# A two-layer mixture-of-experts kernel: where the shared experts of the last two token segments stand, and how the last result is stored

## The chip, the cores and the metric

The kernel runs on one core of one Trainium2 chip, in one launch. The metric is the device time of that launch in microseconds; smaller is better. The kernel before takes 1428.38 us (median of 3 runs, 1427.42 to 1430.12).

A core has TensorE (PE, matmuls and transposes; PEld is its weight load), VectorE (DVE), ScalarE (ACT), GpSimd (POOL) and SyncE (SP), each with a queue of instructions of its own that it works off in order, and 16 DMA engines. Here SP issues the loads and the output stores, ACT the writes of finished pages, and POOL the indirect transfers.

## The reference, cut to what matters

The input is x of 4 x 1024 x 256 (4096 tokens, D = 256), all in float32. Four blocks follow one another, each on a layer norm of x and added to x: an RWKV mixer, a mixture of experts, a retention mixer, and the same mixture of experts again with the same weights. The change lies in the last block:

```python
logits = flat @ router_w
scores = jax.nn.softmax(logits, axis=-1)
_, topk_idx = jax.lax.top_k(logits + router_bias, K)             # K = 4 of E = 64
...
g = silu(einsum('nd,edf->nef', flat, wg));  u = einsum('nd,edf->nef', flat, wu)
routed = einsum('ne,nef,efd->nd', comb, g * u, wd)               # F = 64 per expert
sg = silu(einsum('nd,sdh->nsh', flat, swg)); su = einsum('nd,sdh->nsh', flat, swu)
shared = einsum('nsh,shd->nd', sg * su, swd)                     # 2 x 256 hidden, every token
return (routed + shared)
```

So each token passes four of 64 small routed experts and, besides, two shared experts that see every token.

## The kernel before, in words

**Tiling.** The 4096 tokens are 8 segments (`NSEG`) of 512, each 4 tiles of 128 (`TT`). x stays in SBUF for the whole kernel as eight tiles `xs[i]` of 128 x 4 x 256. The routed experts work on pages: 128 rows that belong to one expert. Tokens are sent to rows of a buffer `sent` in HBM by indirect DMAs; a pair of pages at a time is loaded, worked on and written to a buffer `made`; then each tile of tokens gathers its four rows from `made` and adds them to x with their weights. In the usual case, which this input takes, there are 83 pairs, numbered 0 to 82.

**The routed steps** (`routed`). Step p issues `load(p)` (on SP: 256 KB of rows `rx_f` and two times 192 KB of weights `rw_f`), `up` of pair p-2 (four transposes `rt_f`, L542, copied by VectorE, L546), `mid` of pair p-3 (eight matmul records `rg_f`, L554; silu on ScalarE, L559; product on VectorE, L562) and `down` of pair p-4 (`rp_f`, L574; copied out on ScalarE, L581, and written to `made` by a DMA on ACT's queue, L582). Rows and weights have 6 buffers, finished pages 4.

**The shared experts** (`shared(i)`). Six steps per segment: four `up` (each 4 matmul records `g_f` and 4 `u_f`, L457, silu on ScalarE, L462, product on VectorE, L463) and two `down` (each 16 records `o_f`, L470, and an add to two tiles of x on VectorE, L475). The hidden activations `sh_f` have one buffer, the result of a `down` has one PSUM buffer, and `g_f`, `u_f` and `rg_f` share four.

**The gathers** (`gather`, `gathers`). For each tile four indirect DMAs on POOL (`gy_f`, L606), and `LAG` = 7 positions later four adds on VectorE (L617). A gather waits for the latest "beat", one of the products or copies L463, L546 and L562 that was emitted before it (`on_beat`), and for the pages it may read. Segment i may read the pages up to `until(i)`: 33, 38, 43, 51, 59, 67, 75 and 83 pairs.

**The order.** `track(steps, lo, hi)` spreads a list of steps evenly over positions from `lo` to `hi`, where a position is a step of the routed loop, and `merge` sorts all steps by position and emits them. The builder then orders the instructions of each engine within what the dependencies allow; the adds of a gather and the gathers keep the order in which they were emitted. In `second_layer` the shared experts of segments 0 to 2 are already done (`BESIDE` + `FILL` = 3). Those of segments 3 to 6 are spread over positions 0.5 to n - 4 with n = 83, those of segment 7 over n - 3 to n + 11. A store of a segment (L1253) stands behind the adds of its last tile. The gathers of segment 7 stand at 86.5 to 94.5, its adds at 93.5 to 101.5.

Of the kernel before, what the change touches and what calls it, by code (L numbers as in the profile page):

```python
# [25 lines left out]
TT = SEG // P  # L26
# [22 lines left out]
def track(steps, lo, hi):  # L49

    return [(lo + (hi - lo) * n / len(steps), step) for n, step in enumerate(steps)]


def merge(*tracks):

    for _, step in sorted((s for t in tracks for s in t), key=lambda s: s[0]):
        step()
# [3 lines left out]
def hybrid_kernel(ctx: ExitStack, tc: tile.TileContext, a: dict, out: bass.AP):  # L61
    nc = tc.nc
    B, T, _ = a["x"].shape
    N = B * T
    NSEG = N // SEG
# [27 lines left out]
    def seg_dram(t, i):  # L93
        b, s = divmod(i, SPB)
        return t[b, s * SEG : (s + 1) * SEG, :].rearrange("(t p) d -> p t d", p=P)
# [5 lines left out]
    def bank(tag, name, shape=None):  # L101
# [9 lines left out]
    xs = [const.tile([P, TT, D], F32, name=f"x{i}") for i in range(NSEG)]  # L111
# [7 lines left out]
        out=upper, in_=ones, compare_op=ALU.is_ge, fill=0.0, base=-1,  # L119
# [41 lines left out]
    PACE, LAG = 2, 7.0  # L161
# [1007 lines left out]
    BESIDE, FILL = 0, 3  # L1169
# [14 lines left out]
    def first_layer(until):  # L1184
# [16 lines left out]
        with right("turned") as pt:  # L1201
# [38 lines left out]
            with tc.tile_pool(name="pr2", bufs=2, reuse_waits="tile") as pr:  # L1240
                f2.in_order(
                    lambda u: second_layer(f2, pr, u), pairs_until if until is pairs_until else None
                )
        arm.close()

    def second_layer(f2, pr, until):

        side, stores = [], []
        for i in range(BESIDE + FILL, NSEG - 1):
            side += f2.shared(i)  # L1250
        gathers = f2.gathers(pr, until)
        for i in range(NSEG):
            store = lambda i=i: nc.sync.dma_start(out=seg_dram(out, i), in_=xs[i])  # L1253
            stores.append((gathers[2 * i + 1][-1][0] + 0.1, store))

        n = until(NSEG - 1)
        merge(
            f2.routed(pr, until), *gathers, stores, track(side, 0.5, n - 4),
            track(f2.shared(NSEG - 1), n - 3, n + 4 + LAG),
        )  # L1260

    f1.in_order(first_layer)
# [63 lines left out]
```

## Time and profile before

| what | value |
|---|---|
| median of 3 runs | 1428.38 us (1427.42 to 1430.12) |
| profiled execution, its time | 1426.64 us |
| its span from first to last instruction | 1424.7 us |
| mean granted TensorE clock | 0.954 |
| TensorE busy | 1260.2 us, 88% of the span |
| VectorE, ScalarE, GpSimd busy | 994.2, 738.6, 529.9 us |
| first matmul of the second layer's routed pairs | 1107.43 us |
| last matmul record | 1398.13 us, 3.72 us long |
| last gather issued, last add | 1415.38 us, 1418.22 us |

Times inside an execution count from the start of its span. "Busy" is the time in which an engine works on an instruction; a wait counts as idle and is put down to what ended it. Names such as `rg_f<-rxT_f,rw_f` read "output <- inputs" with the buffer numbers left out, and L554 is line 554 of the kernel before. In tables by stretches of time each engine has its busy time and, in brackets, its number of instructions; behind them stand the granted clock as a share of full speed, the mean busy share of the 16 DMA engines (slightly over 1 where packets overlap) and the bytes moved.

### The profile page before, as it was taken

The page shows a single profiled execution, that of the slowest core. Times are in us where ns is not written, and L with a number is a line of the kernel's source. Part 1 is how long each engine was busy: PE and PEld are TensorE (multiplying, and loading weights), DVE is VectorE, ACT ScalarE, POOL GpSimd, SP SyncE. Part 2 cuts the span into 40 slices and gives each one's busy share as a digit, 9 for nine tenths or more (in the row PEclk, how much of TensorE's full clock was granted, in tenths as well). Part 3 has the DMA queues.
Part 4 walks back from the last instruction along what each step waited for, and adds up shares of the span by engine and source line. Part 5 has one row for each costly group of instructions (what it writes and reads, how often), then busy time and mean ns, then how long its engine had stood idle before and what let it go on. Part 6 is the DMA issues. An engine that isn't in the chain of part 4 may idle for free. (4 is left out here: it accounts for less than half of the span.)

```text
span 1424.7 us, 23821 instructions
## 1 busy us (share of the span) xinstructions
PE 1260.2 (88%) x7872; PEld 891.4 (63%) x7872; DVE 994.2 (70%) x2510; ACT 738.6 (52%) x1422; POOL 529.9 (37%) x536
## 2 busy tenths in 40 slices
PE   6789999999389979998998999799997899999993
PEld 2455555556277767776776666566464687777772
DVE  6999989998355547775777788866673355486664
ACT  7989888973134455555654463433331234454440
POOL 0043255536400155432334105536717000376565
PEclk9999999999789999998999999799999899999997
DMA  9985931112399996765552101212202898999984
GB/s 350 403 254 74 297 115 60 60 37 82 123 310 349 336 331 211 235 206 195 164 187 91 36 31 68 74 38 79 100 16 103 260 318 278 324 384 378 363 310 128
DMA packets 192297, 276.26 MB, mean 194 GB/s; under 512 B 53795, under 2 KB 119718, under 8 KB 192166
## 3 DMA queue, kind: packets, MB, share of 16 engines
q1 hardware_dynamic: 143686, 163.98, 36.1%
q0 software_dynamic: 24576, 67.14, 14.2%
q10 hardware_dynamic: 23904, 43.53, 8.1%
q8 instruction: 65, 1.06, 0.3%
q14 instruction: 66, 0.54, 0.1%
HBM read 166.05 MB, written 121.11 MB: 202 GB/s over the span
## 5 line engine op out<-in xcount | busy, mean ns | idle before, releaser
L429 POOL DMA_INDIRECT sent<-xn_f,to_f x256 | 278.2, 1087 | 415.3 <-issue 192.9
L606 POOL DMA_INDIRECT gy_f<-made,to_f x256 | 248.6, 971 | 468.9 <-DVE rh_f L562 143.3
L554 PE MATMUL rg_f<-rxT_f,rw_f 128*128 128x128 f32 x1328 | 186.6, 283 | 8.4 <-DVE rxT_f L546 2.9
L554 PEld LDWEIGHTS rg_f<-rxT_f,rw_f 128*128 128x128 f32 x1328 | 165.9, 194 | 19.7 <-DVE rxT_f L546 11.6
L559 ACT ACTIVATE rs_f<-rg_f 64x256 f32<-64x256 f32 x166 | 62.4, 376 | 218.9 <-PE rg_f L554 187.4
L542 PE MATMUL rt_f<-ident,rx_f 128*128 128x128 f32 x664 | 107.2, 285 | 45.3 <-DMA rx_f<-sent 41.5
L574 PE MATMUL rp_f<-rw_f,rh_f 64*128 64x128 f32 x1328 | 137.9, 300 | 6.9 <-DVE rh_f L562 3.6
L546 DVE COPY rxT_f<-rt_f 128x512 f32<-128x512 f32 x166 | 114.2, 688 | 39.5 <-PE rt_f L542 37.9
L581 ACT COPY ry_f<-rp_f 128x256 f32<-128x256 f32 x266 | 92.8, 374 | 90.8 <-DMA made<-ry_f 40.3
L617 DVE SCALAR_TENSOR_TENSOR x<-gy_f,w_f,x 128x256 f32<-128x256 f32 x256 | 122.1, 480 | 14.6 <-DMA gy_f<-made,to_f 10.8
L457 PE MATMUL g_f<-xnT_f,f_swg 128*128 128x512 f32 x256 | 130.7, 627 | 0.6 <-ACT sh_f L462 0.6
L470 PE MATMUL o_f<-f_swd,sh_f 128*128 128x256 f32 x512 | 121.5, 385 | 8.2 <-DVE sh_f L463 4.2
L574 PEld LDWEIGHTS rp_f<-rw_f,rh_f 64*128 64x128 f32 x1328 | 102.1, 186 | 34.9 <-ACT ry_f L581 8.7
L457 PE MATMUL u_f<-xnT_f,f_swu 128*128 128x512 f32 x256 | 122.2, 595 | 0.7 <-DVE sh_f L463 0.7
L542 PEld LDWEIGHTS rt_f<-ident,rx_f 128*128 128x128 f32 x664 | 76.2, 144 | 69.4 <-issue 34.1
L562 DVE TENSOR_TENSOR rh_f<-rg_f,rs_f 64x256 f32<-64x256 f32 x166 | 70.6, 426 | 64.9 <-ACT rs_f L559 61.8
L470 PEld LDWEIGHTS o_f<-f_swd,sh_f 128*128 128x128 f32 x512 | 94.9, 190 | 30.0 <-DVE sh_f L463 6.7
L683 PE MATMUL rvk<-xnT_a,rvk 128*128 128x512 f32 x192 | 91.5, 623 | 7.9 <-DVE xnT_a L240 7.4
L1060 DVE TENSOR_TENSOR pm<-sc,decay 128x512 f32<-128x512 f32 x128 | 83.8, 681 | 8.3 <-PE sc L1039 7.1
L463 DVE TENSOR_TENSOR sh_f<-u_f,sh_f 128x512 f32<-128x512 f32 x64 | 43.7, 685 | 62.5 <-PE u_f L457 56.3
L462 ACT ACTIVATE sh_f<-g_f 128x512 f32<-128x512 f32 x64 | 38.0, 596 | 90.7 <-PE g_f L457 50.9
L457 PEld LDWEIGHTS u_f<-xnT_f,f_swu 128*128 128x128 f32 x256 | 48.1, 191 | 57.1 <-issue 52.6
(238 smaller groups left out, 2178.0 us busy)
## 6 DMA issues: line engine op xcount, KB each, us to landing
rw_f<-wx SPq DMA_DIRECT2D x332, 192.0 KB
rx_f<-sent SPq DMA_DIRECT2D x166, 256.0 KB
made<-ry_f ACTq DMA_DIRECT2D x166, 256.0 KB
sent<-zeros SPq DMA_DIRECT2D x7, 2048.0 KB
sent<-zeros SPq DMA_DIRECT2D x1, 10240.0 KB
x<-in_x_dram SPq DMA_DIRECT2D x8, 512.0 KB
wx<-in_wg_dram SPq DMA_DIRECT2D x2, 2048.0 KB
sent<-xn_f,to_f POOLq DMA_INDIRECT x256
```

The costliest lines, as they stand in the source:

```text
L429: ins = nc.gpsimd.indirect_dma_start(out=rows_sent[: pairs_until(i) * 2 * P, :], out_offset=bass.IndirectOffsetOnAxis(ap=st["to"][:, c : c ...
L457: nc.tensor.matmul(ps, lhsT=w[:, k, s], rhs=self.xnT[i][:, k, :], start=(k == 0), stop=(k == KC - 1),)
L470: nc.tensor.matmul(o[:, t, :], lhsT=st["h"][:, c, s], rhs=self.weights[2][:, c, :], start=(c == 0), stop=(c == NS - 1),)
L542: nc.tensor.transpose(tp[:, k, j, :], s["x"][:, j, k * P : (k + 1) * P], ident)
L546: beat(nc.vector.tensor_copy(out=xT, in_=tp))
L554: nc.tensor.matmul(gu[:, j, :], lhsT=s["w"][:, j, k * 2 * F : (k + 1) * 2 * F], rhs=s["xT"][:, k, j, :], start=(k == 0), stop=(k == KC - 1),)
L574: nc.tensor.matmul(yp[:, j, :], lhsT=s["h"][r, j, :], rhs=s["w"][r, j, WD:], start=True, stop=True,)
L581: copy(out=y[:, :, c * P : (c + 1) * P], in_=yp)
L606: ins = nc.gpsimd.indirect_dma_start(out=got[t][:, k, :], out_offset=None, in_=rows_made[: ready[t] * 2 * P, :], in_offset=bass.IndirectOf ...
L617: tc.keep_in_program_order(nc.vector.scalar_tensor_tensor(out=xs[i][:, t, :], in0=got[t][:, k, :], scalar=s["w"][:, c : c + 1], in1=xs[i][ ...
L683: nc.tensor.matmul(ps, lhsT=rvk[:, k, lo : lo + P], rhs=st["xnT"][:, k, :], start=(k == 0), stop=(k == KC - 1),)
L1060: ins = nc.vector.tensor_mul(out=pm, in0=ch[j]["sc"][g], in1=decay.rearrange("p (k g b) n -> p g k b n", k=KC, b=2)[:, g],)
```

## The change

In the second layer only. The shared experts of segment 6 leave the spread-out list (which then holds segments 3 to 5, 18 steps instead of 24, over the same positions) and get positions n + 2 to n + 6, 85 to 89, around and behind the last steps of the routed loop. Those of segment 7 move from n - 3 ... n + 11 to n + 6 ... n + 10, 89 to 93. The store of the last segment becomes four stores of one tile (128 KB) each, every one behind the adds of its tile; the other segments are still stored whole.

```diff
         side, stores = [], []
-        for i in range(BESIDE + FILL, NSEG - 1):
+        for i in range(BESIDE + FILL, NSEG - 2):
             side += f2.shared(i)
         gathers = f2.gathers(pr, until)
         for i in range(NSEG):
-            store = lambda i=i: nc.sync.dma_start(out=seg_dram(out, i), in_=xs[i])
-            stores.append((gathers[2 * i + 1][-1][0] + 0.1, store))
+
+            each = [slice(t, t + 1) for t in range(TT)] if i + 1 == NSEG else [slice(0, TT)]
+            for t in each:
+                store = lambda i=i, t=t: nc.sync.dma_start(
+                    out=seg_dram(out, i)[:, t, :], in_=xs[i][:, t, :]
+                )
+                stores.append((gathers[2 * i + 1][t.stop - 1][0] + 0.1, store))
+
 
         n = until(NSEG - 1)
         merge(
             f2.routed(pr, until), *gathers, stores, track(side, 0.5, n - 4),
-            track(f2.shared(NSEG - 1), n - 3, n + 4 + LAG),
+            track(f2.shared(NSEG - 2), n + 2, n + 6), track(f2.shared(NSEG - 1), n + 6, n + 10),
         )
```

In the list of changes the work is the same: the same matmuls, adds and bytes, three more output transfers.

## The prediction

> **What bounds the kernel now.** I read four views. First the page, for which part of the span the change touches: the last nine slices (from about 1104 us) are the second layer.
>
> ```profile
> PE 1260.2 (88%) x7872; PEld 891.4 (63%) x7872; DVE 994.2 (70%) x2510; ACT 738.6 (52%) x1422; POOL 529.9 (37%) x536
> ...
> PE   6789999999389979998998999799997899999993
> ...
> DMA  9985931112399996765552101212202898999984
> GB/s 350 403 254 74 297 115 60 60 37 82 123 310 349 336 331 211 235 206 195 164 187 91 36 31 68 74 38 79 100 16 103 260 318 278 324 384 378 363 310 128
> ```
>
> TensorE and the DMA engines are both full there, and both go idle together in the last slice. Which of the two would give way is the question. Second, the table of busy time in stretches of 10 us (PE, PEld, DVE, ACT, POOL, then clock, DMA share, GB/s):
>
> ```profile
> 1160.00:1170.00 10.00, 10.00 (x83) 8.07 (x82) 6.34 (x13) 4.61 (x12) 0.00 (x0) 1.00 0.92 293
> ...
> 1260.00:1270.00 10.00, 10.00 (x72) 7.31 (x71) 9.37 (x20) 5.23 (x14) 7.85 (x8) 1.00 1.05 392
> ...
> 1290.00:1300.00 10.00, 7.58 (x44) 5.40 (x44) 4.31 (x9) 4.10 (x11) 7.56 (x9) 0.83 1.03 368
> ...
> 1340.00:1350.00 10.00, 8.57 (x60) 7.33 (x59) 6.12 (x13) 4.48 (x12) 5.58 (x7) 1.00 1.00 337
> ...
> 1400.00:1410.00 10.00, 1.85 (x9) 1.29 (x7) 6.76 (x15) 0.00 (x0) 7.87 (x8) 0.80 0.54 158
> ```
>
> Three regimes. Until about 1220 TensorE is full and the DMA moves 260 to 330 GB/s. From there (gathers have begun) to 1370 TensorE is still full and the DMA moves 355 to 392, with two dips; the thirteen rows from 1240 to 1370 have a mean of 375.5 GB/s and a share between 1.00 and 1.06. From 1392 TensorE runs dry. Third, the chain of waits at the end:
>
> ```profile
> 1387.88 0.89 PE rg_f L554 x8
> ...
> 1393.89 3.47 PE o_f L470 x16
> ...
> 1398.50 0.95 POOL gy_f L606
> ...
> 1415.38 2.75 DMA gy_f<-made,to_f
> ...
> 1418.22 0.48 DVE x L617
> ```
>
> After the last pair's pages are made, sixteen gathers of the last segment go out, one every 1.25 us, then an add and a store: the end is POOL's, and TensorE idles in it. Fourth, TensorE's own timeline there, with the work that the change moves:
>
> ```profile
> 1386.00 1.88 PE L457 MATMUL u_f<-xnT_f,f_swu 128*128 128x512 f32 x4
> 1387.72 1.05 PE L554 MATMUL rg_f<-rxT_f,rw_f 128*128 128x128 f32 x8
> 1388.70 0.72 PE L574 MATMUL rp_f<-rw_f,rh_f 64*128 64x128 f32 x8
> 1389.35 1.13 PE L457 MATMUL g_f<-xnT_f,f_swg 128*128 128x512 f32 x2
> ...
> 1398.13 3.72 PE L470 MATMUL o_f<-f_swd,sh_f 128*128 128x256 f32 x16 [0.78 <-DVE x L475]
> ```
>
> The row at 1387.72 is `rg_f` of the last pair (82). From its start to the end of the span is 37.0 us. I use it as the mark: the change makes the way to it shorter and the way from it longer.
>
> **The way to the mark, if TensorE sets it.** One `up` of a shared expert costs 2 x 1.72 us (the spacing of its groups), one `down` 3.45 (16 matmuls in 3.47), a segment 20.7. In the order in which TensorE gets its instructions, seven `up` and two `down` that now stand ahead of the mark stand behind it afterwards: 7 x 3.44 + 2 x 3.45 = 31.0 us. Of these 10.3 (one `up`, two `down`) are already gone at pair 40, whose `rg_f` starts at 1239.64, because 18 shared steps instead of 24 are spread over the same pairs. TensorE alone would reach the mark at 1356.7.
>
> **If the DMA sets it.** The trace's DMA packets have the weights of pair 40 landed at 1233.2 and those of pair 82 at 1375.5, with 53.0 MB moved between (48.8 in the thirteen rows, 4.2 at the edges). The weights lie 6.4 us ahead of `rg_f` at pair 40 and 12.2 at pair 82. Afterwards pair 40 is there at 1222.9 if the first regime gives its 10.3: there the DMA has room: a pair takes 3.19 us now (`rp_f` of pair 10 at 1151.1, of pair 33 at 1224.4), a shared step every 4.36 instead of 3.27 positions takes 0.26 off, and 293 x 3.19/2.93 = 319 GB/s is less than the 355 and more seen later. In the second regime TensorE wants 148.1 - 20.7 = 127.4 us for these 42 pairs; 53.0 MB in that is over 410 GB/s, more than any row. So TensorE catches up with the loads, and the pages and gathers of the three pairs by which it now trails move in that stretch too: 3 x 576 KB (256 written, 256 gathered, 64 stored) = 1.7 MB. 54.7 MB at the mean of 375.5 take 145.7: mark at 1368.6, 19.1 earlier instead of 31.0. Bounds: at 372.4, this stretch's own 53.0 MB in 142.3 us, 1369.8; at 392, the best row, 1362.4; at TensorE's own pace 1356.7. I take the mean and not the best row because what makes the dips (a page write that waits for an output store, a store that holds SP's queue) stays in the program.
>
> **The way from the mark.** By the new order: `rg_f` 0.98, `rp_f` 0.65, two `up` 6.88, the last `rp_f` 0.65, two `up` 6.88, two `down` with the 0.78 wait for their one PSUM buffer 7.68, four `up` 13.76 less one matmul of 0.43 that fits in that wait, two `down` 7.68; 0.32 until VectorE starts: 45.1. VectorE's queue has all sixteen adds of the last segment behind the second `down`'s add: 0.61 + 16 x 0.50 = 8.6. Then the store: 6.0 from the last add to the end now (1418.70 to 1424.70), with 512 KB in packets from 1419.64 to 1421.32; a quarter of them takes 0.42, so 4.7. The bounds for that store are 4.3 (no packets) and 6.0 (nothing saved). Sum 58.4, which is 21.4 more than now.
>
> What hides what: the last pair's page lands some 3.6 us after its `rp_f` (1391.05 to 1394.6), so sixteen gathers at 1.25 plus 2.75 would be over about 27 us behind it; TensorE and its adds take 36 and more, so the gathers no longer end anything. POOL's last six gathers now wait for the last `up` (a gather waits for the latest beat), and still land 6 us before their adds are due. The adds of segment 6 stand between the multiplies of the shared `up` in VectorE's queue; their gathers go out pair by pair some 10 us ahead, as now. SP is moved past nothing: the stores of segments 5 to 7 stand behind the last load in both programs, four issues of 0.4 us instead of one, three of them during the adds. ACT's `silu` of the moved `up` (0.60) lies beside matmuls of 3.44.
>
> **Sum.** +21.4 - 19.1 = +2.3. To this comes the clock: after the 2.33 us wait before 1295.94 the row's clock is 0.83, and eight `rp_f` took 1.60 instead of 0.72 and four `g_f` 3.27 instead of 1.98, 2.2 us in all. A TensorE that waits for loads will meet this about once more (bounds: none, and three times): +4.5. The profiled execution took 1426.64 for a span of 1424.7, the median of the runs is 1.74 above that; on the median 1428.38 this gives 1432.9.
>
> Two rules set beside these rows. The Trainium skill, "DMA: Bandwidth & Descriptors", section "Where 436 GB/s comes from", puts the ceiling at 435 GB/s by the ports and at about 358 where HBM binds: by 358 the mark would be at 1375.7 and the sum +9.4, by 435 TensorE would set the pace and the sum be -9.6. The rows of 375 to 392 already exceed the lower figure, so the measurement decides. "TensorE: Matmul & The Clock Gate", section "What's actually happening", lets the clock fall only after an idle window of about 3.4 us; by that the short waits for loads would cost no clock and the sum would be +2.3, but the row shows a fall after a wait of 2.33.
>
> **The rivals.** (A) The DMA engines carry more than they are asked for now, and it gets faster. For: rows of 392 stand next to each other, and the loads land 6 to 12 us before use. Against: the share does not rise above 1.06. It decides at 54.7 MB / (1366.3 - 1222.9) = 381 GB/s; at 392 the end is 3.9 earlier (1424.5), at TensorE's pace 9.6 earlier (1418.8). (B) The first regime gives nothing, because a DMA share of 0.9 is already its limit at 293 GB/s. Against: the row of 1150 to 1160 moves 373. It would cost up to 10.3 more: 1443. (C) VectorE stalls in the tail: an add of segment 6 whose gather is late stands before a multiply that frees TensorE's PSUM banks. Each microsecond late is one more; with four gathers late (5 us) 1438. For it speaks that POOL runs without a break from 1372 on now.
>
> **Chances.** My case 0.50 (1427 to 1437; slower 0.41, within 0.09), A 0.32 (faster 0.28, within 0.04), B 0.11 and C 0.07 (slower). Within means 0.2%, 2.9 us, about what a measurement of this kernel can tell from no change. So faster 0.28, same 0.13, slower 0.59. The range leaves out TensorE's full pace at one end and the whole of B at the other: 1420 to 1441.
>
> **What would show it.** Right: the last `rg_f` near 1368, 54 to 60 us before the end; GB/s between 1230 and 1360 like today's mean; gaps on TensorE before `rg_f` that loads end; all sixteen `x` adds of the last segment without gaps behind the last L475; a last chain through `o_f` and `u_f` in place of POOL. Wrong: rows above 385 throughout and the mark before 1364 (A), pair 40 not earlier than 1236 (B), L463 waits in the tail ended by a gather (C).

## The result and the profile after

| | kernel before | changed kernel |
|---|---|---|
| median of 16 runs each | 1431.18 us (1419.49 to 1441.13) | 1435.76 us (1431.78 to 1440.81) |
| profiled execution, its time and span | 1426.64 us, 1424.7 us | 1434.38 us, 1432.6 us |
| `rg_f` of pair 40, of pair 82 (the mark) | 1239.64, 1387.72 us | 1229.9, 1371.37 us |
| from the mark to the end of the span | 37.0 us | 61.3 us |
| last `x` add ends, from there to the end | 1418.70 us, 6.0 us | 1425.47 us, 7.2 us |

The ratio is 1.0044, 95% interval 1.0025 to 1.0064: the changed kernel is slower by 6.3 us (3.6 to 9.2) by the ratio and by 4.6 us between the medians, where 4.5 were forecast. A ratio, here and below, leaves out the executions in a slower state and so is not quite that of the two medians (1.0032 here). The two profiled executions lie 7.7 us apart; that of the kernel before is 4.5 us under its median here, that of the changed kernel 1.4 under its own. The sums below are made between the profiles.

First the page of the changed kernel, its 40 slices.

```profile
PE   6789999999298879998998999789996999988895
...
DMA  9986931112599986766453011112203899999952
GB/s 349 403 252 79 295 108 59 59 41 78 169 314 335 318 305 211 234 209 214 145 188 90 25 46 67 59 49 86 81 33 112 298 315 342 369 386 360 368 192 69
```

In the kernel before, TensorE and the DMA engines went idle together in the last slice. Now the DMA engines go quiet in the last two slices (192 and 69 GB/s) while TensorE works on there (its digits are 9 and 5, where the last one was 3): the shared experts stand behind the last loads. The table in stretches of 10 us (PE, PEld, DVE, ACT, POOL, then clock, DMA share, GB/s) shows the same and one thing more.

```profile
1160.00:1170.00 10.00, 9.70 (x88) 8.38 (x85) 6.25 (x13) 5.04 (x14) 0.00 (x0) 1.00 0.99 340
...
1260.00:1270.00 10.00, 9.82 (x65) 7.06 (x64) 6.82 (x14) 5.20 (x14) 7.56 (x9) 1.00 1.06 396
...
1300.00:1310.00 10.00, 8.40 (x48) 7.18 (x48) 4.25 (x9) 3.23 (x10) 4.21 (x5) 0.67 1.01 349
...
1350.00:1360.00 10.00, 6.65 (x62) 5.69 (x60) 5.34 (x11) 4.03 (x12) 6.32 (x7) 1.00 1.05 384
...
1400.00:1410.00 10.00, 10.00 (x27) 4.88 (x26) 3.66 (x7) 1.79 (x3) 3.50 (x4) 1.00 0.19 51
```

The first regime has become faster (340 GB/s in this row where it had 293; the seven rows from 1150 to 1220 have a mean of 325 after 303). The second moves about what it moved before, but TensorE is no longer full in it: it waits, and the row from 1300 has a mean granted clock of 0.67. In the trace's record of the clock this mean is half the clock from 1299.91 to 1303.32 and again from 1306.74, and the full clock between. The last row is the new tail, TensorE alone. TensorE's own timeline shows the mark and the end of the tail:

```profile
1371.37 1.16 PE L554 MATMUL rg_f<-rxT_f,rw_f 128*128 128x128 f32 x8
1372.46 0.89 PE L574 MATMUL rp_f<-rw_f,rh_f 64*128 64x128 f32 x8
...
1413.19 3.72 PE L470 MATMUL o_f<-f_swd,sh_f 128*128 128x256 f32 x16 [0.78 <-DVE x L475]
```

VectorE's timeline from there has the second `down`'s add and then all sixteen adds of the last segment in one block:

```profile
1416.94 0.69 DVE L475 TENSOR_TENSOR x<-o_f,x 128x512 f32<-128x512 f32 x1 [3.81 <-PE o_f L470]
1417.55 7.91 DVE L617 SCALAR_TENSOR_TENSOR x<-gy_f,w_f,x 128x256 f32<-128x256 f32 x16
```

No gather is waited for. POOL's chain at the end of the kernel before is gone, and its place is taken by the matmuls.

Where TensorE waits in the middle, the chain of waits (start, length, what was waited for) runs through transfers:

```profile
1288.10 8.35 DMA rx_f<-sent
1296.47 7.22 DMA rw_f<-wx
1303.77 5.07 DMA made<-ry_f
1308.91 4.15 DMA made<-ry_f
```

I had expected TensorE to wait for its weights. It does not: by the packets, the weights of pair 60 have landed at 1292.7 and its `rg_f` starts at 1299.3, those of pair 82 at 1366.0 and 1371.4. Nor is a transfer named in the list of its waits from pair 40 to the mark (what waited, for what; us in total, times, longest), of which these are the first three lines:

```profile
PE rp_f L574 <- DVE rh_f L562: 6.2, 4, 3.4
PE rt_f L542 <- DVE rxT_f L546: 4.9, 6, 1.9
PE rt_f L542 <- ACT ry_f L581: 0.9, 1, 0.9
```

What waits for transfers is ScalarE, in order, as its timeline around two of the stalls shows (ACTq is the issue of a page write):

```profile
1303.77 0.33 ACTq L582 DMA_DIRECT2D made<-ry_f  x1
1304.14 0.38 ACT L559 ACTIVATE rs_f<-rg_f 64x256 f32<-64x256 f32 x1 [4.11 <-PE rg_f L554]
...
1358.25 0.33 ACTq L582 DMA_DIRECT2D made<-ry_f  x1
1358.63 0.38 ACT L559 ACTIVATE rs_f<-rg_f 64x256 f32<-64x256 f32 x1 [4.78 <-DMA out_dram<-x]
```

The page write at 1303.77 goes out when the weight load issued at 1296.47 has landed (7.22 us, the second line of the chain), the one at 1358.25 when an output store has. The trace shows why: the transfers of SyncE and ScalarE take eight completion semaphores in turn, in the order of the program, and a transfer waits for the one eight before it, whatever that is. (The page write at 1303.77 has the semaphore of that weight load, whose last update came at 1303.69.) The `silu` of the next pair (`rs_f`) stands behind the page write on ScalarE, `rh_f` on VectorE and `rp_f` on TensorE behind that. The first of the two stalls is put down to `rg_f`, which had ended at 1300.6: a label names what came last by the profile, and is not always what was waited for.

There is a second path, by the copies `rxT_f`, which stand on VectorE behind adds that wait for their gathers. One of TensorE's waits for them is this (1.30 us):

```profile
1270.80 0.88 DVE L617 SCALAR_TENSOR_TENSOR x<-gy_f,w_f,x 128x256 f32<-128x256 f32 x2 [1.06 <-DMA gy_f<-made,to_f]
1271.71 0.69 DVE L546 COPY rxT_f<-rt_f 128x512 f32<-128x512 f32 x1
1272.46 0.66 PE L542 MATMUL rt_f<-ident,rx_f 128*128 128x128 f32 x4 [1.30 <-DVE rxT_f L546]
```

### The profile page after: what moved, and what is told of

The parts are those of the page before. It is cut to its first block, busy times and chain, and to the rows that moved or that the text cites. A ratio compares the mean times of both kernels' runs of the same rounds, so it can differ in the third digit from the quotient of the medians.

```text
span 1432.6 us, 23824 instructions
## 1 busy us (share of the span) xinstructions
PE 1261.7 (88%) x7872; PEld 894.3 (62%) x7872; DVE 994.1 (69%) x2510; ACT 737.5 (51%) x1422; POOL 525.6 (37%) x536
## 3 DMA queue, kind: packets, MB, share of 16 engines
q1 hardware_dynamic: 143734, 163.98, 36.1%
## 5 line engine op out<-in xcount | busy, mean ns | idle before, releaser
L554 PE MATMUL rg_f<-rxT_f,rw_f 128*128 128x128 f32 x1328 | 189.8, 286 | 10.0 <-DVE rxT_f L546 3.6
L554 PEld LDWEIGHTS rg_f<-rxT_f,rw_f 128*128 128x128 f32 x1328 | 168.8, 197 | 20.9 <-DVE rxT_f L546 11.4
L559 ACT ACTIVATE rs_f<-rg_f 64x256 f32<-64x256 f32 x166 | 62.4, 376 | 212.8 <-PE rg_f L554 169.9
L574 PE MATMUL rp_f<-rw_f,rh_f 64*128 64x128 f32 x1328 | 142.2, 302 | 12.8 <-DVE rh_f L562 6.5
L574 PEld LDWEIGHTS rp_f<-rw_f,rh_f 64*128 64x128 f32 x1328 | 105.0, 189 | 42.9 <-ACT ry_f L581 14.7
L457 PE MATMUL g_f<-xnT_f,f_swg 128*128 128x512 f32 x256 | 126.2, 609 | 0.6 <-ACT sh_f L462 0.6
L563 ACT COPY rh_f<-rh_f 64x256 f32<-64x256 f32 x166 | 66.8, 403 | 32.8 <-DVE rh_f L562 24.2
```

The costliest lines, as they stand in the source:

```text
L457: nc.tensor.matmul(ps, lhsT=w[:, k, s], rhs=self.xnT[i][:, k, :], start=(k == 0), stop=(k == KC - 1),)
L554: nc.tensor.matmul(gu[:, j, :], lhsT=s["w"][:, j, k * 2 * F : (k + 1) * 2 * F], rhs=s["xT"][:, k, j, :], start=(k == 0), stop=(k == KC - 1),)
L574: nc.tensor.matmul(yp[:, j, :], lhsT=s["h"][r, j, :], rhs=s["w"][r, j, WD:], start=True, stop=True,)
```

## The experiments

Two theories stand against each other for the stretch from pair 40 to the mark, where 20.7 us of TensorE's work were taken out and only 6.7 us were gained. R: the bytes set it; what TensorE no longer asks for in time is filled by the rate of the DMA engines. Q: ScalarE's queue sets it, by waits that have to do with the order of the transfers and not with how many bytes they move. A third question is the store, from whose four parts 1.3 us were to come.

The first eight kernels ran on two other chips, where the kernel before took 1583.88 us (35 runs, beside E1, E2, E6 and E9) and 1610.85 us (29 runs, beside E3, E4, E5 and E7). There the bytes moved from pair 40 to the mark are carried at 269 to 296 GB/s, by the packets that start in the stretch, against 360 (before) and 369 (changed) in the first profiles. So ratios are compared within a group, not times, and the intervals are wide. The profiles of these eight hold 1663 to 2102 semaphore updates in that stretch, those of the other six kernels 4021 to 4269: what ended a wait is not safely read from them.

**E1 and E2: the two parts of the change alone.** E1 is the kernel before with the new stores, E2 the changed kernel with the old one:

```diff
 # E1 on the kernel before; E2 is its reverse on the changed kernel
-            store = lambda i=i: nc.sync.dma_start(out=seg_dram(out, i), in_=xs[i])
-            stores.append((gathers[2 * i + 1][-1][0] + 0.1, store))
+            each = [slice(t, t + 1) for t in range(TT)] if i + 1 == NSEG else [slice(0, TT)]
+            for t in each:
+                store = lambda i=i, t=t: nc.sync.dma_start(
+                    out=seg_dram(out, i)[:, t, :], in_=xs[i][:, t, :]
+                )
+                stores.append((gathers[2 * i + 1][t.stop - 1][0] + 0.1, store))
```

> The kernel before with the last segment's store in four tiles and nothing moved. If the transfer of the last store sets the end, as the prediction took it (6.0 us from last add to end become 4.7), it is 1.3 us faster than before (ratio 0.999). Rival: in both traces SyncE's final semaphore steps come 2.7 to 3.8 us behind its last branch and instruction-queue packets stand between, so the program's end and not the store sets the time; then the split gains nothing, 0 to +1.2 us (ratio 1.000 to 1.001), and the time from last add to end stays at 5.9 to 7.2 us.

> The changed kernel with the last segment stored whole, so only the shared experts are moved. If the split saved its 1.3 us, this is 1.3 us slower than the changed kernel (ratio to before about 1.0053); if the split saves nothing, it equals the changed kernel (1.003 to 1.0044). In both the last pair's rg_f stands near 1371 and 58 to 62 us before the end.

E1: 1589.12 us, ratio 1.0002 [0.9959, 1.0045]. E2: 1590.51 us, 1.0037 [1.0000, 1.0074]. The runs point to the move for the loss, though the interval of E2 ends at no change; that of E1 is too wide to say anything of one microsecond. From the last add to the end E1 has 5.8 us, where 4.7 were expected if the transfer sets the end, and E2 6.2 (6.0 in the kernel before, 7.2 in the changed one): see the part on the end of the program below.

The two profiles also show where the move gives and takes there. From pair 40 to the mark E1 needs 192.2 us and E2 171.0; up to pair 40 (from pair 0) 128.7 and 121.7; from the mark to the end 35.5 and 66.5. That is 28.2 us gained and 31.0 lost, on a chip where the whole stretch runs at another speed.

**E6: only the last segment is moved.** Segment 6 stays in the spread-out list; segment 7 goes to the first place behind the pairs.

```diff
-        for i in range(BESIDE + FILL, NSEG - 2):
+        for i in range(BESIDE + FILL, NSEG - 1):
...
-            track(f2.shared(NSEG - 2), n + 2, n + 6), track(f2.shared(NSEG - 1), n + 6, n + 10),
+            track(f2.shared(NSEG - 1), n + 2, n + 6),
```

> Segment 6 stays spread over the pairs as before; segment 7 alone stands at n + 2 to n + 6; stores in tiles. Three up (10.3 us of TensorE) leave the way to the mark, the way from it grows from 37.0 to about 42 (two up 6.9 ahead of the last page, then page, sixteen gathers at 1.25, 2.75, add, 6.0). If TensorE sets the way to the mark: 5 us faster than before (0.9965). If the gather regime gives back only half or less of what TensorE is spared, as in the changed kernel (16.3 of 31.0): 0 to +1 us (1.000 to 1.001).

1586.08 us, 1.0021 [0.9984, 1.0058]. From pair 40 to the mark 183.2 us, from the mark 48.8: against E1, which has the same stores, 9.5 us gained up to the mark and 13.3 lost behind it. Beside the 28.2 and 31.0 of the whole move this is a third of the gain and less than half of the loss; the interval does not tell the sum from nothing. The way from the mark was expected at about 42 us. It is longer because the last fourteen gathers go out only from 1557.27 us on: they wait for the latest beat, the product (L463) of the last shared `up`, which starts at 1556.31, and GpSimd then sets the end of this kernel.

**E9: the last segment's shared experts spread further,** so that its adds could come between them.

```diff
-            track(f2.shared(NSEG - 2), n + 2, n + 6), track(f2.shared(NSEG - 1), n + 6, n + 10),
+            track(f2.shared(NSEG - 2), n + 2, n + 6), track(f2.shared(NSEG - 1), n + 6, n + 12.5),
```

> The changed kernel with segment 7's shared steps at n + 6 to n + 12.5, which puts the first tile's four adds between the two down adds on VectorE. If the sixteen adds behind TensorE's last matmul are on the path, 2.0 us faster than the changed kernel (12 adds of 0.50 left behind it): ratio to before about 1.003. If something else sets the end (gathers, store): no change against the changed kernel, 1.0044.

1590.82 us, 1.0030 [0.9992, 1.0068], not told from E2. From the last matmul to the last add it is 6.6 us in place of 8.6, the 2.0 that were expected, but from the mark to the end 69.8 in place of 66.5, most of it in the last pair's own steps right behind the mark (TensorE waits 3.84 and 2.73 us there before the two halves of an `rp_f`) and in a longer end of the program (7.5 us). The tail is TensorE's 41.4 us of shared experts, and no order of the adds shortens those.

**E3 and E7: the page writes leave ScalarE.** In the changed kernel (E3) and in the kernel before (E7) SyncE issues them in the second layer:

```diff
-                nc.scalar.dma_start(out=made[p * P : (p + 1) * P], in_=y)
+                (nc.sync if self.name == "f2_" else nc.scalar).dma_start(out=made[p * P : (p + 1) * P], in_=y)
```

> The changed kernel with the second layer's finished pages written from SyncE's queue instead of ScalarE's: same bytes, same transfers. Theory R (rate): between the first gather and the last load the DMA engines' rate of 375 GB/s sets the pace; then nothing changes: last rg_f at 1369 to 1373, ratio to before about 1.004. Theory Q (queue): what TensorE loses there is ScalarE standing still behind a page write that waits for another transfer to land (4.0 us at 1294, 4.1 at 1304, 4.8 at 1358, and the cold clock after it); then these gaps go, the last rg_f comes at 1360 to 1366 and the kernel is 5 to 10 us faster than the changed one (ratio to before 0.997 to 1.001).

> The same for the kernel before: the second layer's pages written from SyncE's queue. Theory R: no change (0.999 to 1.001). Theory Q: the ScalarE waits for output stores and pages of this stretch (5.8 and 3.2 us) go, 3 to 6 us faster (0.996 to 0.998). A loss would say that SyncE's loads, which now stand behind the page write, come too late.

E3: 1637.91 us, 1.0192 [1.0134, 1.0250]. E7: 1619.68 us, 1.0091 [1.0049, 1.0133]. Neither theory had a loss of 1.9%. The waits of SyncE's queue in E3 between pair 40 and the mark say what happened (what waited, for what; us in total, times, longest):

```profile
SPq L582 <- ACT ry_f L581: 33.8, 14, 7.1
```

This wait can be read here, as SyncE goes on 0.03 us after a copy of ScalarE's each time. The page write now holds the loads behind it until its pair is computed. The weights land 6.2 us ahead of their `rg_f` on the mean of the pairs from 40 on (12.2 in E4, which leaves the page writes on ScalarE, in the same group), at the least 1.0, and the stretch from pair 40 to the mark takes 192.7 us (169.9 in E4). A page write has to wait somewhere, and the queue with the loads is the worse place. So the edit took one wait away and made another, and says nothing for R or against Q. (A loss by late loads is the third outcome that the expectation of E7 names.)

**E4 and E5: the output stores come late,** behind the last load, so that no page write can wait for one. Here E4 on the changed kernel; E5 is the same on the kernel before. The loads and stores are held in the order of the program, by lines left out here.

```diff
+        late = until(NSEG - 1) + 4.5
...
-                stores.append((gathers[2 * i + 1][t.stop - 1][0] + 0.1, store))
+                stores.append((max(late, gathers[2 * i + 1][t.stop - 1][0] + 0.1), store))
```

> The changed kernel with all output stores behind the last load, and the loads in program order: six stores of 512 KB leave the stretch of the gathers and move into the tail, where the DMA moves 50 GB/s. Theory R: 3.1 MB less at 375 GB/s, the last rg_f 8 us earlier (near 1363). Theory Q: the stalls behind a store's landing (4.8 us and the cold clock after it) go, the others stay, 5 to 7 us earlier. Both: ratio to before about 0.999. No gain would tell against both.

> The same for the kernel before. Theory R: TensorE sets the pace there, so only the few stalls go, 0 to 3 us faster, and the tail has room for 3.1 MB beside the gathers (134 to 158 GB/s now). Theory Q: ScalarE's 5.8 us behind output stores and the 2.2 us of cold clock go, 4 to 8 us faster (0.994 to 0.997).

E4: 1610.19 us, 1.0020 [0.9988, 1.0052]. E5: 1605.12 us, 0.9986 [0.9941, 1.0031]. Each is within its interval of what its kernel does without the edit. The times decide nothing: 0.999, which both theories gave for E4, lies just inside its interval, and that of E5 holds what either gave. The stretch from pair 40 to the mark shows no gain (169.9 in E4 beside 171.0 in E2, 194.4 in E5 beside 192.2 in E1, on the other chip of the two). But in E4 the stores go out from 1526.3 us on, behind the last load and still ahead of the mark at 1536.4. Where they are gone, from `rg_f` of pair 40 to the issue of the last load, E4 takes 159.3 us with 45.7 MB and E2 159.3 with 48.2. As far as two chips can be compared, 2.5 MB less bought nothing there, which speaks against R on the slower chips. The stores stand in the label of the longest stall of the first profile, but that they set the stretch is not shown.

**E10 to E13: fewer bytes at the same transfers.** In the second layer a weight load brings a third of its columns; for the other two thirds the matmuls read a tile that stays, so the weights of two experts serve all (the edit of the matmuls is left out here).

```diff
+                few = self.name == "f2_"
+                if few and not p:
+                    self.kept = pool.tile([P, 2 * WD + 2 * P - 4 * F], F32, tag="rk", bufs=1, name=f"rk_{nm}")
...
+                c = 2 * F if few else WD + P
                 for j, e in enumerate(got):
                     nc.sync.dma_start(
-                        out=w[:, j], in_=wx[bass.ds(e, 1)].rearrange("e p c -> p (e c)")
+                        out=w[:, j, :c], in_=wx[bass.ds(e, 1)].rearrange("e p c -> p (e c)")[:, :c]
                     )
```

E10 is this on the changed kernel, E11 on the kernel before; E12 and E13 are the two kernels unaltered. All four ran on one chip.

> The change with fewer bytes at the same transfers: in the second layer each weight load brings 512 bytes a partition in place of 1536 (a third of the columns); the matmuls on the other two thirds read two experts' weights kept in SBUF, so the routed experts of that layer are computed with the wrong weights there. TensorE's, ScalarE's, VectorE's and GpSimd's instructions, the order, and the waits of a transfer on the one eight before it stay. The bytes of the 42 pairs from 40 to 82 go from 53 to about 42 MB. R (bytes by the DMA's rate set that stretch): at 375 GB/s 42 MB take 112 us, less than TensorE's own 127.4, so rg_f of pair 82 comes 127 to 130 us after that of pair 40 (141.4 in the changed kernel's first profile, 171.0 with the whole store on the slower chip); against the same edit on the kernel before (e11) this kernel is 6.7 us faster (31.0 freed less 24.3 longer from the mark), ratio between the two 0.996. Q (ScalarE's queue, which waits at a page write for the landing of an earlier transfer, sets it, whatever the bytes): the stalls before rs_f of 4 us and more stay, the stretch is 138 or more, and this kernel is slower than e11 by 0.2 to 0.4%.

> The same edit on the kernel before. R: TensorE is the bound there, rg_f of pair 82 comes 148 us after that of pair 40 (148.1 in its first profile; 192.2 in the slower chip's profile of it with the store in tiles), and the kernel gains on the kernel before by what that stretch exceeded 148 on this chip: nothing where it was 148, up to 44 us where it was 192. Q: the stretch stays within 5 us of what it is in the kernel before on this chip.

> The change unaltered, for its profile and time beside the two runs with few weights on the same chip. Both theories: 1.002 to 1.006 of the kernel before. On a chip like the first one, pair 40 to pair 82 takes 141 us and the way from the mark 61; where the DMA is slower, 170 and 64 to 67 as with the whole store.

> The kernel before unaltered, for its profile on the same chip. Both theories: pair 40 to pair 82 takes 148 us and the way from the mark 37 on a chip like the first; 192 and 36 where the DMA is slower, as with the store in tiles.

The kernel before took 1431.51 us there (23 runs).

| | median, ratio to the kernel before | pair 40 to the mark | of it TensorE without a matmul | GB/s in it | mark to the end |
|---|---|---|---|---|---|
| before (E13) | 1431.51 us | 145.9 us | 5.9 us | 366 | 37.0 us |
| changed (E12) | 1434.36 us, 1.0022 [0.9993, 1.0051] | 138.3 | 12.0 | 376 | 61.2 |
| before, few weights (E11) | 1423.63 us, 0.9950 [0.9926, 0.9974] | 141.4 | 2.2 | 300 | 36.1 |
| changed, few weights (E10) | 1419.10 us, 0.9911 [0.9885, 0.9938] | 126.6 | 6.0 | 324 | 59.2 |

The median in the first row is that of the 23 runs; the stretches of every row come from one profiled execution each. GB/s are the bytes of the packets that start in the stretch, over its length.

In this stretch it is R's result. With the same instructions in the same order on TensorE (but for four records), ScalarE, VectorE and GpSimd, but 11 MB fewer bytes, it takes 126.6 us (127 to 130 were expected by R, 138 or more by Q), 14.8 less than in the kernel before with few weights, where the full kernels have 7.6 between them. In the full kernels the bytes cost the changed kernel 11.7 us of this stretch (138.3 less 126.6) and the kernel before 4.5 (145.9 less 141.4). The 7.2 us between these two are more than what the change loses. Each of these lengths is one execution's; two of the same kernel on different chips differ by 2.2 and 3.1 us (148.1 and 145.9 before, 141.4 and 138.3 changed). In the first regime the bytes cost nothing: from pair 0 to pair 40 E10 takes 116.7 us and E12 116.8, E11 127.1 and E13 126.5.

Not quite everything else is the same, as E10's expectation had it. There is one load more ahead of pair 0, and by the traces SyncE issues some loads and stores in another order in E10 than in E12, and in E11 than in E13, so that some page writes wait for another transfer. That both pairs lose stalls (below) speaks for the bytes; a run with that order held was not made.

The whole times say less. The changed kernel is now the faster of the two, 1419.10 to 1423.63 us, and the two ratios stand at 0.9961 to each other, where R gave 0.996; with the two intervals taken as independent this reaches from 0.9925 to 0.9997. But 2.1 us of it have nothing to do with the stretch: E10 ends 5.1 us after its last add and E12 7.1, for a reason that the part on the end of the program looks at, while E11 and E13 have 5.9 and 6.0. Without them the sign is not settled; Q's 1.002 to 1.004 lies outside either way.

R missed one number: the kernel before was to gain nothing where its stretch took 148 us, and gained 4.5 us there and 0.5% in all. It too seems to be held by its bytes a little; TensorE was not quite full. And R's 127.4 us were not TensorE's own pace, as the stretch that they were taken from held 6.0 us of waits: in E10 TensorE has matmul records in 120.6 of the 126.6 us.

How the bytes act is seen in the waits. From pair 40 to the mark TensorE mainly waits so in the changed kernel (E12):

```profile
PE rp_f L574 <- DVE rh_f L562: 5.8, 6, 1.8
PE rt_f L542 <- DVE rxT_f L546: 4.4, 8, 1.8
```

With few weights (E10, where these lines have other numbers) its wait for `rh_f` is gone:

```profile
PE rt_f L550 <- DVE rxT_f L554: 5.2, 5, 3.7
```

And in the kernel before on the same chip (E13):

```profile
PE rt_f L542 <- DVE rxT_f L546: 4.2, 4, 2.2
PE rp_f L574 <- DVE rh_f L562: 1.5, 2, 1.1
```

For ScalarE the labels of such a list mislead. The longest wait that E10's list puts down to a landing, 3.80 us, is 0.95 us of it; then TensorE is busy with a shared `down`, and `rg_f` comes late:

```profile
1335.56 3.72 PE L470 MATMUL o_f<-f_swd,sh_f 128*128 128x256 f32 x16
1337.85 0.33 ACTq L595 DMA_DIRECT2D made<-ry_f  x1
1340.22 0.39 PE L562 MATMUL rg_f<-rxT_f,rk_f 128*128 128x128 f32 x2
1340.65 0.38 ACT L570 ACTIVATE rs_f<-rg_f 64x256 f32<-64x256 f32 x1 [3.80 <-DMA made<-ry_f]
```

So I take the stalls at the page writes themselves: from the end of what ScalarE did before to the semaphore instruction that lets the write go, where the last update of that semaphore lies within 0.08 us ahead of it.

| | stalls of ScalarE at a page write, pair 40 to the mark | times | longest |
|---|---|---|---|
| before (E13) | 24.5 us | 22 | 2.9 us |
| changed (E12) | 33.9 | 26 | 2.8 |
| before, few weights (E11) | 9.8 | 14 | 3.2 |
| changed, few weights (E10) | 9.5 | 17 | 1.2 |

They go with the bytes, by 24.4 us in the one pair and 14.7 in the other, and TensorE's wait for `rh_f`, the end of that line, goes from 5.8 us to none. Most of such a stall costs nothing: in E13 24.5 us of it stand beside 5.9 us without a matmul. So Q is right about one place where the time is lost and wrong about what sets its size: ScalarE waits for landings, and the landings are late where the bytes are many (the ten rows from 1240 to 1340 us have a DMA share of 1.02 to 1.07 in E12 and of 0.85 to 1.04 in E10).

What is late next in E10 is the second path, the gathers. In the row from 1270 TensorE is busy for only 6.54 us; VectorE waits for gathers there, and the copy behind its adds comes late:

```profile
1278.57 0.52 DVE L630 SCALAR_TENSOR_TENSOR x<-gy_f,w_f,x 128x256 f32<-128x256 f32 x1 [1.84 <-DMA gy_f<-made,to_f]
1279.50 0.48 DVE L630 SCALAR_TENSOR_TENSOR x<-gy_f,w_f,x 128x256 f32<-128x256 f32 x1 [0.41 <-DMA gy_f<-made,to_f]
1280.02 0.69 DVE L554 COPY rxT_f<-rt_f 128x512 f32<-128x512 f32 x1
1280.76 0.66 PE L550 MATMUL rt_f<-ident,rx_f 128*128 128x128 f32 x4 [3.73 <-DVE rxT_f L554]
```

E10's loads are also shorter each, and not only fewer bytes in all; no run separates the two. An edit that gave the queue more than eight transfers in flight, which would separate the wait from the bytes, was not tried.

**The end of the program.** From the last add to the end of the span it is 6.0 us in the kernel before (6.0 in E13), 7.2 in the changed one (7.1 in E12), and 5.1 in E10 and in E4, which have the same four stores. The split did what it should as far as the transfer goes: the last packet of the store lands 1.5 us after the last add in place of 2.6, and the first closing step of SyncE (a semaphore instruction behind the program's last line) starts at 3.1 us in place of 4.2. But in the changed kernel and in E12 there is a gap of 2.15 us between the second and the third of these steps, in E9 one of 2.4; in E10 and E4 there is none, in E3 one of 1.9 us lies before the sixth step, and in E1 and E6 one of 1.3 and 1.0 us before the 15th. Transfers of 8 KB on the instruction queue lie beside these gaps, but they lie at the same places where there is no gap (2.97 and 3.62 us after the last add in the changed kernel, 3.00 and 3.62 in E10). What the steps wait for was not tested and stays open.

## Why the prediction was right, point by point

- **The sum.** +4.5 us were forecast; +6.3 (3.6 to 9.2) were measured by the ratio and +4.6 between the medians. That the medians agree to a tenth is luck: taken as a time, the forecast of 1432.9 lies 2.9 us under the 1435.76, and between the profiles, from which the terms were worked out, it is +8.0 (spans): 2.5 us of the store, 0.6 at the mark and 0.4 in the tail more than predicted, on top of 4.5. In E12 and E13 17.4 us are gained up to the mark, from pair 0, and 24.3 lost behind it; the 6.9 between them lie within what the runs give (-1.0 to +7.3 us, 2.85 between the medians). The spans of these two profiles are 15.5 us apart because that of E12 comes to pair 0 8.6 us later, in a part that the change leaves as it is. One profiled execution cannot price a change of this size.
- **The first regime gives its 10.3.** `rg_f` of pair 40 came 9.7 us earlier, and 9.7 again from pair 0 on between E12 and E13 (7.0 between E1 and E2 on a slower chip). Rival B is out.
- **The mark at 1368.6, and 2.2 for the clock.** 1371.37 was measured, against 1370.8 with the clock. The size is right. E10 and E11 show how much of what is missing from the 31.0 us is due to the bytes: from pair 0 to the mark the change gains 17.4 us between E13 and E12 and 25.2 between E11 and E10, so 7.8 of the 13.6 us. The step in words failed: "a TensorE that waits for loads" waits for ScalarE and VectorE, which wait for landings, and in the list of TensorE's waits from pair 40 to the mark no transfer is named. The clock was one term that came larger: TensorE's records cover 142.1 us of the 148.1 before and 128.1 of the 141.4 after, so 14.0 us less where 20.7 us of work left; the 6.7 between them is longer records. By the trace's record of the clock at most 5.1 of that are clock: half the clock was granted in four stretches of 3.41 us (from 1299.91, 1306.74, 1337.46 and 1361.35), after one before (from 1296.69). So the clock fell three more times, the upper bound that was given, and not once more. The waits, 13.3 us instead of 6.0, are the rest. Two terms that were priced as 11.9 of rate and 2.2 of clock came out as 7.3 of waits and 6.7 of longer records. That their sum hit is partly luck.
- **The dips.** They were put down to a page write that waits for an output store, and to a store that holds SyncE's queue. E4 and E5 put the stores behind the last load and gained nothing that could be told. The page write is the right place, beside the gathers on VectorE's path; the transfer that it waits for may be any.
- **The tail, 45.1 and 8.6.** From the mark to the end of the last add 54.1 us, against 53.7. All sixteen adds stand in one block of 7.91, no gather is late (rival C is out), and VectorE's wait of 3.81 before the last L475 is TensorE's `down`. (The line for rival C, that GpSimd runs without a break from 1372 on, was misread: in the kernel before it waits 1.31 us ahead of 1388.85 and 1.99 ahead of 1395.78.)
- **The store, 4.7 in place of 6.0.** This is the term that was mis-sized: 7.2. The transfer shortened by the 1.1 us that its packets explain, but the end of the program is not the transfer's end, and the row of before that I took it from held both.
- **Rival A, the DMA carries more.** It decided at 381 GB/s. The stretch moved 369 in the first profile and 376 in E12; single rows reached 396, and others in between fell to 342. It was near: at E12's 376 the loss (2.85 us) has an interval that includes no change.

Two rules can be held against these rows. The rows of 384 to 396 GB/s again exceed the 358 of the Trainium skill, "DMA: Bandwidth & Descriptors", section "Where 436 GB/s comes from"; of the means over the stretch in kernels with all their bytes only those of the slower chips, 269 to 296, lie under it. By "TensorE: Matmul & The Clock Gate", section "What's actually happening", the clock falls after an idle window of about 3.4 us. In TensorE's timeline of the changed kernel the longest wait ahead of the row at 0.67 is 1.86 us, and its matmuls are slow from the next group on (1.23 us for eight `rp_f`, 0.76 ahead of it):

```profile
1296.17 0.76 PE L574 MATMUL rp_f<-rw_f,rh_f 64*128 64x128 f32 x8
1298.79 0.66 PE L542 MATMUL rt_f<-ident,rx_f 128*128 128x128 f32 x4 [1.86 <-DVE rxT_f L546]
1299.28 1.34 PE L554 MATMUL rg_f<-rxT_f,rw_f 128*128 128x128 f32 x8
1300.56 1.23 PE L574 MATMUL rp_f<-rw_f,rh_f 64*128 64x128 f32 x8
```

So here the measurement decides against the rule as worded, and short waits have to be priced with the clock that follows them.

## What to carry to other kernels

Work that is moved behind the last transfers costs its whole length there, and frees in front of them only what the engine was the bound for: ask of the stretch that it leaves how many bytes it would have to move in the time that remains. Where an engine issues transfers in its own queue, look at its waits for landings: here they grew with the bytes (9.5 and 33.9 us in E10 and E12), so a rate was a usable price for them even though TensorE was not seen waiting for its data. And a store at the end of a program should be priced by what follows its landing, not by its packets.

## What the runs showed of the hardware that I had not expected

- The kernel before took 1431, 1584 and 1611 us on different chips. The slower ones carried 269 to 296 GB/s in the second regime, with the weights of the pairs from 40 on landed 12 to 14 us ahead of their `rg_f` on the mean in E1, E2, E4 and E5 (6 to 8 in the four profiles of the full kernels where the kernel before took 1431 us): the loads were not what was late there either.
- 11 MB of bytes for which TensorE was never seen to wait cost the changed kernel 11.7 us in this stretch, and the kernel before 4.5.
- Between the closing steps of a program there can be 2.2 to 2.4 us, the same in two executions of the same program (7.18 and 7.13 us from the last add to the end), and none in E10, a program that differs only ahead of them.
- TensorE's clock fell to half for 3.41 us after single waits of under 2 us (1.86 us ahead of 1299.91, 1.53 ahead of 1337.46; 1.82 ahead of 1281.07 in E12).
